# The order in which the tiles of an edge table are taken: falling width, or narrow ones among wide ones

## The chip, the cores and the metric

The kernel runs on one core of one Trainium2 chip. The metric is the device time of one execution in microseconds. Engines are called as the profile calls them: PE (TensorE, matmul), DVE (VectorE), ACT (ScalarE), POOL (GpSimd) and SP (SyncE). Each engine works through its own queue in the order in which the program was written; an instruction that waits holds everything behind it on that engine.

## What is computed

Two layers of a graph network run on `x` of 16 batches, 1024 nodes and 256 features, with one adjacency matrix `adj` of 1024 x 1024 for all batches. At most one entry in 60 of `adj` is not zero (the table below has room for 17,280 of 1,048,576).

```python
# layer 0: attention over all nodes
feats = x @ W1.T                                   # 16 x 1024 x 256
f1 = feats @ W2 + b2
coefs = softmax(leaky_relu(f1[:, :, None] + f1[:, None, :]) + adj)
h = coefs @ feats + bias2 + x
# layer 1: a score for each pair (u, v), weighted by adj
pre_u, pre_v = h @ W1[:256], h @ W1[256:]
S = sigmoid(relu(pre_u[:, :, None] + pre_v[:, None, :] + b1) @ W2 + b2)
a = einsum('buv,bud->bvd', S * adj, h)
m = einsum('uv,bud->bvd', adj, h) * h
z = beta1 * h + beta2 * (a @ Wa + ba) + beta3 * (m @ Wm + bm)
```

A score `S[u, v]` is multiplied by `adj[u, v]`, so it is needed only where `adj` is not zero. The kernel computes scores for these edges alone.

## The kernel before

Everything runs in `edge_layers`. PE does the dense work from end to end: features, attention and messages for batch after batch, and at the end the sum over `u` weighted by the scores. The scores are made beside it, by POOL, DVE and ACT, in three groups of batches (`GROUPS`: 5, 5 and 6 batches). They lie back in DRAM between the two: scores are scattered into `sa_d`, a dense 1024 x 1024 table for each group that was cleared before, and read from there as `sat` for the last matmuls.

**The table of edges.** In the first 340 us the kernel sorts the edges into pieces: up to eight edges of one row `u`, one piece to a partition, 128 pieces to a tile. There are 21 tiles. Tile `t` has `WIDTHS[t]` columns: thirteen tiles of width 8, then 7, 6, 5, 4, 3, 3, 2, 1. A column of a tile is a slot: 128 edges, one on each partition. `SLOTS` lists all 135 slots as pairs (tile, column), and this list sets the order in which every group works.

**One slot** (number `k` of a group) goes through these steps:

- `fetch` (lines 1215 to 1232): at a tile's first column, POOL issues an indirect gather of `gu`, the 128 rows `u` of `pu_d` (L1219), which then serve all columns of the tile; for every slot it issues a gather of `gv`, the rows `v` of `pw_d` (L1226). A row has 272 numbers of four bytes for each batch of the group, 5440 bytes with five batches.
- `compare` (L1255): DVE takes the maximum, and for a second half the minimum, of `gv` and `gu`; two instructions to a slot.
- `sums` (L1269): ACT adds up each batch's 272 numbers, one instruction to a batch. In the last group, every eighth slot is summed by DVE instead (L1266).
- `gates` (L1277, ACT) and L1296 (DVE) finish the scores of some 16 slots at a time.
- `scatter` (L1235): POOL scatters the 128 finished scores of a slot. Scatters wait in a list, `late`, and one or two follow each fetch.

**The rings.** `gv` has five buffers in the first two groups and six in the last, and `gu` has two in every group. The first two groups share one pool, so their rings go on across the border; the last group has a pool of its own. A new `gu` may be gathered only when L1255 has finished the last slot of the tile that held its buffer before. `AHEAD` is three slots in the first two groups and four in the last: the fetch of slot `k + AHEAD` is issued with slot `k`.

**The order.** A small timetable (`Timetable`) sets each instruction's place in its engine's queue. It gives PE's work model times, and all other work is placed relative to these. `scores` spreads a group's 135 slots evenly between two such times. The fetches with which a group begins are placed 15 us before its first slot, that is before the last fetch of the group before it:

```python
for k in range(len(SLOTS)):
    time = start + k * (end - start) / len(SLOTS)

    def first(k=k):
        for n in range(AHEAD[g]) if k == 0 else ():
            fetch(g, n)
        if k + AHEAD[g] < len(SLOTS):
            fetch(g, k + AHEAD[g])
        ...
    times.at(time - (15.0 if k == 0 else 0.0), first)
```

On DVE and ACT the instructions of the scores stand between those on which PE depends: L1054 (weights of the attention), L1081 (rows `h`), L1176 and L1195 (messages), L1357 (scores times `adj`), all on DVE, and L969, L1098, L1119 on ACT.

Of the kernel before, what the change touches and what calls it, by code (L numbers as in the profile page):

```python
# [26 lines left out]
W = 8  # L27
WIDTHS = (8,) * 13 + (7, 6, 5, 4, 3, 3, 2, 1)
TILES = len(WIDTHS)
SLOTS = [(t, s) for t, width in enumerate(WIDTHS) for s in range(width)]  # L30
HUB = 32
SEGS = P // HUB
ROUNDS = (11, 10, 6, 5, 4, 4, 4, 4, 4)
# [338 lines left out]
def edge_layers(  # L372
# [835 lines left out]

    PARTS = [16, 32, 48, 64, 80, 96, 112, 124, 131, len(SLOTS)]
    AHEAD = [n - 2 for n in GV]  # L1210
# [4 lines left out]
    def fetch(g, k):  # L1215
        t, s = SLOTS[k]
        if s == 0:
            gu = st["gu", t] = pools["gath", g].tile([P, SIZE[g] * R], F32, name="gu", bufs=2)
            nc.gpsimd.indirect_dma_start(  # L1219
                out=gu,  # L1220
                out_offset=None,
                in_=pu_d[g],
                in_offset=bass.IndirectOffsetOnAxis(ap=key_u[:, t : t + 1], axis=0),
            )
        gv = st["gv", k] = pools["gath", g].tile([P, SIZE[g] * R], F32, name="gv", bufs=GV[g])
        nc.gpsimd.indirect_dma_start(  # L1226
            out=gv,
            out_offset=None,
            in_=pw_d[g],
            in_offset=bass.IndirectOffsetOnAxis(ap=idx_v[:, t, s : s + 1], axis=0),  # L1230
        )

    def scatter(g, lg, i, k):
        t, s = SLOTS[k]
        dma = nc.gpsimd.indirect_dma_start(  # L1235
            out=sa_d[g],
            out_offset=bass.IndirectOffsetOnAxis(ap=idx_s[:, t, s : s + 1], axis=0),
            in_=lg[:, i, : SIZE[g]],
            in_offset=None,
            bounds_check=N * N - 1,  # L1240
            oob_is_err=False,
        )
        tc.declare_no_dep(dma.ins, group=f"sa{g}", reason="edges of their own")
        tc.add_to_no_dep_group(f"sa{g}", dma.ins)

    def by_batch(tile):
        return tile.rearrange("p (g r) -> p g r", r=R)

    def compare(k, half):
# [3 lines left out]
        mv = by_batch(st["gv", k])[:, :, cols]  # L1253
        mu = by_batch(st["gu", SLOTS[k][0]])[:, :, cols]
        nc.vector.tensor_tensor(mv, mv, mu, op)  # L1255
# [23 lines left out]
    def scores(g, start, end, on_vector):  # L1279

        for k in range(len(SLOTS)):
            time = start + k * (end - start) / len(SLOTS)

# [516 lines left out]
```

## Time and profile before

| what | us |
|---|---|
| median of three runs | 2098.32 |
| the three runs | 2111.71, 2086.22, 2098.32 |
| the profiled execution, its own time | 2079.83 |
| its span in the profile | 2078.1 |

From the trace: the first score (L1255) of group 0 begins at 373 us, that of group 1 at 865 us, that of group 2 at 1336 us, and the last score begins at 1875 us. A slot takes some 3.6, 3.5 and 4.0 us in the three groups.

| per core, whole span | count | busy us | mean ns |
|---|---|---|---|
| POOL L1226, gather of gv | 405 | 497.1 | 1227 |
| POOL L1235, scatter of scores | 405 | 504.1 | 1245 |
| POOL L1219, gather of gu | 63 | | 1025 (median) |
| DVE L1255, compare | 810 | 705.8 | 909 |
| ACT L1269, sums | 2058 | 856.3 | 420 |

How to read it: a row of the page has the busy time of an engine and its share of the span. In the 40 slices, each digit is the busy share of one fortieth of the span, in tenths. In the windows view, the columns behind a stretch are its length and then, for PE, PE's weight loads, DVE, ACT and POOL, the busy time with the number of instructions; behind these the granted clock, the share of the DMA engines and GB/s. In the timeline a row has the start, the time taken, the engine, the line, the operation, out<-in, shapes and count, and in brackets how long the engine was idle before it and what ended that.

The profile's times of POOL are those of making a gather's descriptors; the transfer follows. From issue to landing a gather of gv took 7.7 us in the median (4.8 to 15.0), one of gu 6.5 us (4.6 to 10.7).

### The profile page before, as it was taken

The numbers are of one execution on the slowest core, as the hardware profiler recorded it, in microseconds if no ns is written. First come the engines' busy times: TensorE is split into PE (matmuls) and PEld (weight loads), VectorE is DVE, ScalarE is ACT, GpSimd is POOL, SyncE is SP. The second block draws the span as 40 slices with busy tenths as digits, with TensorE's granted clock in tenths as the row PEclk, the third lists the DMA queues.
The fourth block names the chain that finished last, engine by engine and source line by source line (L and its number), as shares of the span: only waits on it lengthen the run. The fifth ranks groups of instructions, "written<-read, shape, count | busy, mean of one in ns | idle before, by whom it ended". The sixth has DMA issues, their size and how long they took to land.

```text
span 2078.1 us, 28958 instructions
## 1 busy us (share of the span) xinstructions
PE 2020.4 (97%) x8577; PEld 1554.9 (75%) x8577; DVE 1566.8 (75%) x2348; ACT 1371.5 (66%) x4842; POOL 1142.4 (55%) x974
## 2 busy tenths in 40 slices
PE   8999999999999999999999999899999999999998
PEld 6888887777786868677888886457677667767887
DVE  7798883677777777677878886578888888884554
ACT  4212222577777868587888777577888888885654
POOL 1121221267676777677777777666777677683000
PEclk9999999999999999999999999999999999999999
DMA  6689886788888889789999999999999999996873
GB/s 220 240 311 343 306 323 235 247 268 288 285 273 270 275 288 297 254 299 308 315 297 318 327 308 310 326 401 399 399 400 370 415 414 405 400 383 254 281 230 123
DMA packets 250007, 644.37 MB, mean 310 GB/s; under 512 B 38642, under 2 KB 139762, under 8 KB 247794
## 3 DMA queue, kind: packets, MB, share of 16 engines
q0 software_dynamic: 82016, 348.87, 47.9%
q1 hardware_dynamic: 132002, 259.36, 34.2%
q10 hardware_dynamic: 35824, 34.22, 4.7%
q8 instruction: 69, 1.13, 0.2%
q14 instruction: 96, 0.79, 0.1%
HBM read 479.56 MB, written 162.92 MB: 309 GB/s over the span
## 4 chain that ended last, share of the span: by engine, by line
PE 61%; DVE 11%; DMA 9%; ACT 8%; issue 7%; POOL 3%; ACTq 0%; POOLq 0%; DVEq 0%
PE pv L1067 18%; PE pp L1105 10%; PE pm L1165 10%; PE pzg L1370 6%; DMA gv<-pw_d,idx_v 5%; ACT gv L1269 5%; PE pf L1013 5%; DVE gv L1255 4%; PE pea L1133 4%; PE pzh L1370 3%; PE pz L1185 2%; ACT apart L1352 2%; POOL sa_d L1235 2%; DMA xh<-in_x_dram 1%; POOL gv L1226 1%
## 5 line engine op out<-in xcount | busy, mean ns | idle before, releaser
L1269 ACT ACTIVATE gv<-gv 128x272 f32<-128x272 f32 x2058 | 856.3, 420 | 313.0 <-DVE gv L1255 204.7
L1255 DVE TENSOR_TENSOR gv<-gv,gu 128x680 f32<-128x680 f32 (+1 forms) x810 | 705.8, 909 | 97.5 <-DMA gv<-pw_d,idx_v 95.5
L1226 POOL DMA_INDIRECT gv<-pw_d,idx_v x405 | 497.1, 1227 | 297.9 <-ACT gv L1269 181.5
L1235 POOL DMA_INDIRECT sa_d<-lg,idx_s x405 | 504.1, 1245 | 135.2 <-issue 108.2
L1067 PE MATMUL pv<-feats,eT 128*128 128x257 f32 x2048 | 465.5, 380 | 2.7 <-DVE eT L1054 2.0
L1165 PE MATMUL pm<-adj_sb,xh 128*128 128x512 f32 x1024 | 452.8, 595 | 2.6 <-DVE xh L1081 2.6
L1067 PEld LDWEIGHTS pv<-feats,eT 128*128 128x128 f32 x2048 | 382.9, 190 | 61.8 <-DVE eT L1054 4.2
L1269 ACT ACTIVATION_READ_ACCUMULATOR gv<-gv 128x1 f32 x2058 | 389.7, 189 | 0.0
L1370 PE MATMUL pzg<-ha_g,apart 128*128 128x256 f32 x1536 | 367.5, 382 | 19.0 <-DVE apart L1357 18.5
L1165 PEld LDWEIGHTS pm<-adj_sb,xh 128*128 128x128 f32 x1024 | 194.3, 191 | 222.4 <-issue 219.8
L1370 PEld LDWEIGHTS pzg<-ha_g,apart 128*128 128x128 f32 x1536 | 290.2, 191 | 77.2 <-DVE apart L1357 29.5
L1352 ACT COPY apart<-sat 128x640 f32<-128x640 f32 (+1 forms) x192 | 264.2, 1394 | 78.0 <-PE pzh L1370 35.5
L1357 DVE TENSOR_TENSOR apart<-apart,adj_sb 128x640 f32<-128x640 f32 (+1 forms) x192 | 165.9, 867 | 123.3 <-ACT apart L1352 123.0
L1105 PE MATMUL pp<-wuv,hT 128*128 128x272 f32 x1024 | 250.5, 395 | 6.7 <-ACT end L1119 3.8
L1105 PEld LDWEIGHTS pp<-wuv,hT 128*128 128x128 f32 x1024 | 194.7, 191 | 53.7 <-issue 6.5
L1054 DVE SCALAR_TENSOR_TENSOR eT<-row,col,grown 128x512 f32<-128x512 f32 x256 | 182.8, 745 | 27.5 <-ACT col L1000 26.8
L852 POOL DMA_INDIRECT table_d<-rec,at x52 | 57.4, 1105 | 248.4 <-DVE rec L845 151.8
L1098 ACT COPY hT<-ph 128x512 f32<-128x512 f32 x96 | 55.1, 575 | 101.0 <-PE ph L1087 100.7
L1133 PE MATMUL pea<-wa,hT 128*128 128x256 f32 x512 | 121.0, 379 | 0.0
L1185 PE MATMUL pz<-wm,mT 128*128 128x256 f32 x512 | 115.7, 379 | 0.0
L1013 PE MATMUL pf<-w1T,xT 128*128 128x257 f32 x512 | 114.1, 380 | 0.9 <-DVE xT L971 0.9
L1370 PE MATMUL pzh<-ha_g,apart 128*128 128x256 f32 x384 | 114.2, 379 | 0.0
(179 smaller groups left out, 1589.0 us busy)
## 6 DMA issues: line engine op xcount, KB each, us to landing
sa_d<-zero SPq DMA_DIRECT2D x128, 512.0 KB, 5.6
sat<-sa_d SPq DMA_DIRECT2D x128, 320.0 KB, 9.5
sat<-sa_d SPq DMA_DIRECT2D x64, 384.0 KB, 4.2
pu_d<-end SPq DMA_DIRECT2D x64, 272.0 KB, 4.3
pw_d<-end SPq DMA_DIRECT2D x64, 272.0 KB, 5.8
ha_d<-ea SPq DMA_DIRECT2D x64, 256.0 KB, 4.9
zb_d<-zb ACTq DMA_DIRECT2D x64, 256.0 KB, 7.8
xh<-in_x_dram SPq DMA_DIRECT2D x15, 1024.0 KB, 13.6
```

Of the source, the lines that this page charges most:

```text
L1013: nc.tensor.matmul(pfs[i], lhsT=st["xT"][:, h, c * P : (c + 1) * P], rhs=w1T[:, h, :], start=(h == 0), stop=(h == H - 1),)
L1054: nc.vector.scalar_tensor_tensor(st["eT", b, k, n][:, i, :], st["row"][:, cols], st["col"][:, j : j + 1], grown[:, j, cols], ALU.max, ALU. ...
L1067: nc.tensor.matmul(pv[:, : D + 1], lhsT=st["eT", b, k, j // 4][:, j % 4, i * P : (i + 1) * P], rhs=st["feats", b][:, j, :], start=(j == 0) ...
L1105: nc.tensor.matmul(pp[:, k, :R], lhsT=st["hTi", b, i][:, h, k * P : (k + 1) * P], rhs=wuv[:, side, h, :], start=(h == 0), stop=(h == H - 1),)
L1133: nc.tensor.matmul(pp[:, k, :], lhsT=st["hTi", b, i][:, h, k * P : (k + 1) * P], rhs=wa[:, h, :], start=(h == 0), stop=(h == H - 1),)
L1165: nc.tensor.matmul(pm, lhsT=held[b][:, c, h * P : (h + 1) * P], rhs=adj_sb[:, c, span], start=(c == 0), stop=(c == C - 1),)
L1226: nc.gpsimd.indirect_dma_start(out=gv, out_offset=None, in_=pw_d[g], in_offset=bass.IndirectOffsetOnAxis(ap=idx_v[:, t, s : s + 1], axis=0),)
L1235: dma = nc.gpsimd.indirect_dma_start(out=sa_d[g], out_offset=bass.IndirectOffsetOnAxis(ap=idx_s[:, t, s : s + 1], axis=0), in_=lg[:, i, : ...
L1255: nc.vector.tensor_tensor(mv, mv, mu, op)
L1269: nc.scalar.activation(one[:, j, :], one[:, j, :], AF.Copy, accum_out=lg[:, i, j : j + 1])
L1352: nc.scalar.copy(apart.rearrange("p g v -> p v g"), sat)
L1370: nc.tensor.matmul(st["pzg", g, vc][j // 4][:, j % 4, :], lhsT=apart[:, j, :], rhs=ha, start=(c == 0 and j % 2 == 0), stop=(c == C - 1 and ...
```

## The change

The order of the tiles in `SLOTS` is written out. In place of falling width, tiles of width 3, 2, 3, 4, 5, 6 and 7 stand between tiles of width 8; tile 20, of width 1, stays last.

```diff
 WIDTHS = (8,) * 13 + (7, 6, 5, 4, 3, 3, 2, 1)
 TILES = len(WIDTHS)
-SLOTS = [(t, s) for t, width in enumerate(WIDTHS) for s in range(width)]
+ORDER = (0, 1, 18, 2, 3, 19, 4, 5, 17, 6, 7, 16, 8, 15, 9, 14, 10, 13, 11, 12, 20)
+SLOTS = [(t, s) for t in ORDER for s in range(WIDTHS[t])]
```

The slots at which a tile begins:

| order | first slots of the tiles |
|---|---|
| before | 0, 8, 16, ... 96 (tiles 0 to 12), 104, 111, 117, 122, 126, 129, 132, 134 (tiles 13 to 20) |
| after | 0, 8, 16, 19, 27, 35, 37, 45, 53, 56, 64, 72, 76, 84, 89, 97, 103, 111, 118, 126, 134 |

The table, the number of slots, gathers and scatters, and the places of all other instructions in the timetable are the same.

## The prediction

> **What bounds the kernel now.** I start with the page: the engine rows, then the slices.
>
> ```profile
> PE 2020.4 (97%) x8577; PEld 1554.9 (75%) x8577; DVE 1566.8 (75%) x2348; ACT 1371.5 (66%) x4842; POOL 1142.4 (55%) x974
> ...
> PE   8999999999999999999999999899999999999998
> ...
> POOL 1121221267676777677777777666777677683000
> ```
>
> TensorE (PE) is busy for 2020.4 of 2078.1 us, so 57.7 us are all that any rearrangement could return. Whatever moves between the other engines counts only as far as it opens or closes a hole in PE. Next, therefore, the windows view, cut where the groups of scores begin, and where slot 104 of 135 comes in each group:
>
> ```profile
> 0.00:373.00 373.00, 361.89 (x1745) 305.62 (x1746) 294.15 (x565) 95.22 (x180) 70.95 (x107) 1.00 0.77 284
> 373.00:740.00 367.00, 367.00 (x1521) 274.42 (x1520) 276.63 (x442) 273.02 (x1144) 239.76 (x202) 1.00 0.84 270
> 740.00:865.00 125.00, 122.37 (x491) 88.97 (x490) 85.62 (x137) 82.12 (x352) 88.72 (x76) 1.00 0.87 294
> 865.00:1216.00 351.00, 342.37 (x1553) 278.37 (x1554) 286.20 (x472) 286.92 (x1186) 259.91 (x219) 0.99 0.90 302
> 1216.00:1336.00 120.00, 116.64 (x424) 76.68 (x424) 70.08 (x112) 74.94 (x328) 90.01 (x76) 1.00 0.94 330
> 1336.00:1751.00 415.00, 398.01 (x1500) 276.38 (x1501) 345.74 (x398) 343.24 (x1214) 286.02 (x217) 0.99 1.01 395
> 1751.00:1876.00 125.00, 117.70 (x471) 86.80 (x471) 109.17 (x125) 108.71 (x362) 94.56 (x67) 1.00 0.99 383
> ```
>
> Length less PE's busy time gives PE's holes: 11.1 us at the start, 0 and 2.6 in group 0, 8.6 and 3.4 in group 1, 17.0 and 7.3 in group 2; 7.6 remain behind 1876, mostly the last stores. The timeline of PE shows the three largest holes in the scores, and all stand at the last slot of a group:
>
> ```profile
> 864.81 3.53 PE L1165 MATMUL pm<-adj_sb,xh 128*128 128x512 f32 x4 [2.63 <-DVE xh L1081]
> ...
> 1339.92 1.12 PE L1087 MATMUL ph<-ident,xh 128*128 128x128 f32 x4 [7.28 <-DVE zb L1195]
> 1342.41 1.12 PE L1087 MATMUL ph<-ident,xh 128*128 128x128 f32 x4 [1.38 <-DVE zb L1195]
> ...
> 1875.36 3.44 PE L1370 MATMUL pzg<-ha_g,apart 128*128 128x256 f32 x8 [2.90 <-DVE apart L1357]
> ```
>
> DVE releases all of them, so DVE's timeline just before is read next. It stood at L1255, waiting for a gather, with PE's operand queued behind:
>
> ```profile
> 862.43 1.64 DVE L1255 TENSOR_TENSOR gv<-gv,gu 128x680 f32<-128x680 f32 x2 [8.37 <-DMA gv<-pw_d,idx_v]
> ...
> 1334.71 3.48 DVE L1255 TENSOR_TENSOR gv<-gv,gu 128x680 f32<-128x680 f32 x4 [14.05 <-DMA gv<-pw_d,idx_v]
> ...
> 1873.57 1.01 DVE L1255 TENSOR_TENSOR gv<-gv,gu 128x816 f32<-128x816 f32 x1 [2.87 <-DMA gv<-pw_d,idx_v]
> ```
>
> Over the whole trace DVE waits 95.5 us in 41 places for gathers. By slot (the n-th pair of L1255), the last nine slots hold 16.0 us of it in group 0, 25.1 in group 1 and 5.0 in group 2. So the narrow end does hurt; but the largest waits are at slot 134, whose tile comes last in both orders.
>
> **The change part by part.** Arithmetic, slots, scatters, bytes and the 63 gathers of gu all stay; only the places of gu's gathers move, and what their ring of two buffers waits for.
>
> *Removed from the end of each group.* From slot 104 on, before begins eight tiles (104, 111, 117, 122, 126, 129, 132, 134); after begins four (111, 118, 126, 134). A gu costs GpSimd 1.03 us plus 0.30 between instructions, and brings 128 rows of 5440 bytes, 0.70 MB (0.84 in group 2). GpSimd is the tight engine there: in 1216 to 1336 it has 90.0 us and 76 gaps of 0.3, 113 of 120 us.
>
> *Group 1 to 2, the largest term.* The timeline of GpSimd:
>
> ```profile
> 1312.48 0.96 POOL L1219 DMA_INDIRECT gu<-pu_d,key_u  x1 [0.30 <-issue]
> ...
> 1322.31 0.96 POOL L1219 DMA_INDIRECT gu<-pu_d,key_u  x1 [0.30 <-issue]
> 1323.58 0.94 POOL L1226 DMA_INDIRECT gv<-pw_d,idx_v  x1 [0.30 <-issue]
> ```
>
> The first is group 2's first gu: its look-ahead (one gu, five gv, written 15 us ahead) is queued before the last fetch of group 1. The second and third are slot 134's own. Its gv lands 11.0 us after its issue, behind 5.0 MB of look-ahead. GpSimd has run without a longer gap since 1282, when DVE held it. Of the gu issued between then and 1323.6, two (tiles 18 and 19; tile 12's takes the place of 17's) disappear: 2 x 1.33 = 2.7 us of issue, or 1.4 MB; the DMA view of 1296 to 1340 shows some 420 GB/s around 1320, so 3.3 us of transfer. The two overlap. I take 3.5 us earlier for slot 134, and about 0.5 us off the second hole: -4. Bounds: -8.7 if both holes go, 0 if the look-ahead alone sets the landing.
>
> *Group 0 to 1.* Here slot 134's gu waits for L1255 of slot 133 in either order (ring of two, with the next group's first gu in between). From the end of slot 133 at 852.7 to the landing at 862.4 are 9.7 us that stay. What goes are the waits before, 4.4 and 3.2 us at slots 131 and 132, which made DVE late. DVE is idle for a quarter of the time anyway and takes back part; of the 2.6 us hole I take 2: -2 (0 to -2.6).
>
> *End of group 2.* Three gu wait there in before (one took 2.66 us of idle and 3.80 of issue at 1836.87); after has two gu, neither held. I take 2 of the 2.9 us hole: -2 (0 to -4.4, with the two holes of 0.6 and 0.7 before it).
>
> *Added among the wide tiles.* A tile behind a narrow one takes the buffer of the tile before the narrow one. Behind width 2 (tile 4, slot 37) its gu waits for slot 34. Groups 0 and 1 issue it three slots ahead, so DVE reaches slot 37 three slots of 3.6 us later, less 1.7 of its own work: 9.1 us. Needed are 1.3 us for gu, 1.0 for the issue of gv, and gv's landing (median 7.7 from issue): about 9.0 to 10. So DVE waits 0 to 2 us. Group 2 asks four slots ahead, and there widths 2 and 3 (slots 37, 19, 56) wait on the slot directly. Nearest rows for what a wait costs PE: 5.44 us of DVE wait at 461.44 opened no hole at all, 4.26 at 1683.41 opened 1.15. I take 0 in groups 0 and 1 (the dense rows are the nearest) and 1 + 0.5 + 0.5 = +2 in group 2; bounds 0 and +9 (2.9, the price at 1875.36, at three places). Group 1's first part gets four more gu, 5.3 us on a GpSimd filled for 260 + 67 of 351 us; I take +1 (-2 to +3). Queued behind a held gu are its gv, the next gv, and scatters nobody waits for until the group ends.
>
> *A rule against it.* The trace has gv landing 7.7 us after issue. The Trainium skill, "DMA: Bandwidth & Descriptors", section "Anatomy of one DMA — SWDGE (gpsimd) path", fits 2.0 us plus bytes over 436e3 per us: an estimate of 3.6 us for 0.70 MB. By that, three slots of look-ahead would cover everything in either order and the sum would be 0. The row shows twice that under load, and 95.5 us of waits.
>
> Sum: -4 - 2 - 2 + 2 + 1 = **-5 us**. The profiled execution took 2079.8 us (span 2078.1 and 1.7 around it), so 2075 by its own measure. That run lies 18 us under the median of the three shown, 2098.3, and 6 under their lowest. On the median: **2093**. The three spread over 25 us, so within 1% (21 us) counts as no change here.
>
> **Rivals.**
> *The handover, not the narrow tiles, makes the holes.* For: slot 134 keeps its place, its look-ahead and its 9.7 us chain. Against: GpSimd shows only 0.3 us gaps before 1312. Then the ends give 0, the inside +0: 2098.
> *Slower: the ring of gu holds GpSimd inside the groups.* Place: slot 37 of each group, 19 and 56 of group 2. Price: 2.9 us of PE each, as at 1875.36, 14.5; less half of the gains, 4: +10, 2108. It decides if the gv behind the held gu lands over about 10 us after the slot it waited for; group 2's landings of 11 us (1862.90 to 1873.57) speak for it, the holeless 461.44 against. To reach 1% each place would have to cost some 5 us.
> *The whole end was a lag of GpSimd.* Then all holes behind slot 120 go: 2.6 + 8.7 + 4.4, and 1.3 at 893, which a late DVE starts: -17, 2081. Against: half the tile starts remain, and DMA runs at 0.99 there.
>
> **How the numbers follow.** Forecast 0.50, handover 0.19, slower 0.20, whole lag 0.11. Range: the terms' bounds give -18 to +16 about 2098, and a median of three whose runs spread over 25 us may itself move by some 10; both ends seldom meet, so 2070 to 2115. Faster by over 1% needs the whole lag and some holes more: 0.08. Slower by over 1% is the outer part of the slower case: 0.11. Within: 0.81.
>
> **What would show it.** Right: the hole at the end of group 1 falls to about 4 us; DVE's waits at slots 128 to 133 vanish; a wait of gu for L1255 appears at slot 37; the sum of DVE's waits for gathers falls from 95.5 to some 75. Wrong: PE holes over 2 us inside a group, or 14 us still at the last slot. The forecast fails most easily if group 1, whose GpSimd is full already, takes up the moved gathers worse than its end did.

## The result, and the profile after

The change makes the kernel a little slower: 2109.73 us in the median of 22 runs (2096.59 to 2115.23), against 2099.42 of 22 runs of the kernel before in the same sessions. The ratio is 1.0041 [1.0026, 1.0056], or +8.6 us [+5.5, +11.8]; the two medians themselves stand 10.3 apart. The forecast was -5.

The two profiled executions stand 31.8 us apart (2111.66 and 2079.83), and only about a quarter of that is the change: the execution of before that was profiled lies under all of its 22 timed runs (lowest 2086.22), that of after near its median. The two traces can't be subtracted, so most readings below were repeated with pairs from one chip.

From the page of after, the engine rows and two slice rows:

```profile
PE 2034.5 (96%) x8577; PEld 1561.5 (74%) x8577; DVE 1565.9 (74%) x2348; ACT 1371.2 (65%) x4842; POOL 1141.8 (54%) x974
...
PE   8999999999999999999889999899999999999998
...
POOL 1122221366677667667667776666677676683000
```

DVE, ACT and POOL work as long as they did, to 1 us. New are two slices with an 8 in PE's row, just behind 1000 us, in group 1. The windows view of after, with the cuts that the prediction used:

```profile
865.00:1216.00 351.00, 325.79 (x1444) 261.23 (x1443) 264.94 (x434) 264.50 (x1100) 248.12 (x205) 0.97 0.86 285
1216.00:1336.00 120.00, 114.79 (x447) 82.67 (x446) 80.88 (x134) 86.98 (x369) 85.31 (x72) 0.97 0.85 293
1336.00:1751.00 415.00, 395.81 (x1457) 268.40 (x1456) 325.85 (x377) 324.06 (x1161) 283.71 (x220) 0.99 1.00 391
1751.00:1876.00 125.00, 119.03 (x477) 88.27 (x476) 111.21 (x128) 111.18 (x367) 90.55 (x68) 1.00 1.02 398
```

Length less PE's busy time gives 25.2 us of holes in 865 to 1216, where before had 8.6. The other rows have 5.2, 19.2 and 6.0, near before's 3.4, 17.0 and 7.3. So the loss arises in the middle of group 1. (After runs some 30 us late by the end, so its own slots are used from here on: slots 35 to 104 of group 1 lie at 979 to 1247 and hold 26.7 us; in before, at 975 to 1216, 7.3.)

At the ends of the groups the change did what it was expected to do. The timeline of PE in after, and of DVE just before, at the end of group 1:

```profile
1368.49 0.81 PE L1088 MATMUL ph<-ident,xh 128*128 128x128 f32 x4 [4.29 <-DVE zb L1196]
1370.98 1.12 PE L1088 MATMUL ph<-ident,xh 128*128 128x128 f32 x4 [1.69 <-DVE zb L1196]
```

```profile
1363.28 3.48 DVE L1256 TENSOR_TENSOR gv<-gv,gu 128x680 f32<-128x680 f32 x4 [14.86 <-DMA gv<-pw_d,idx_v]
```

The hole fell from 7.28 to 4.29 us, though DVE's wait for slot 134 stayed at 14.86 (14.05 in before). At the last slot of group 0 the hole went from 2.63 to 0.6, and at that of group 2 from 2.90 to none.

### The profile page after: what moved, and what is told of

It reads as the page before. It is cut to its first block, busy times and chain, and to the rows that moved or that the text cites. A ratio compares the mean times of both kernels' runs of the same rounds, so it can differ in the third digit from the quotient of the medians.

```text
span 2109.9 us, 28964 instructions
## 1 busy us (share of the span) xinstructions
PE 2034.5 (96%) x8577; PEld 1561.5 (74%) x8577; DVE 1565.9 (74%) x2348; ACT 1371.2 (65%) x4842; POOL 1141.8 (54%) x974
## 4 chain that ended last, share of the span: by engine, by line
PE 53%; DVE 15%; ACT 11%; issue 9%; DMA 8%; POOL 3%; another core or an unknown queue 1%; ACTq 0%; POOLq 0%; DVEq 0%; SPq 0%
PE pv L1068 15%; PE pm L1166 8%; PE pp L1106 7%; PE pzg L1371 7%; ACT gv L1270 7%; DVE gv L1256 7%; DMA gv<-pw_d,idx_v 6%; PE pea L1134 4%; PE pf L1014 3%; PE pzh L1371 3%; ACT apart L1353 2%; PE pz L1186 2%; DVE apart L1358 2%; DVE eT L1055 1%; POOL gv L1227 1%
## 5 line engine op out<-in xcount | busy, mean ns | idle before, releaser
L1256 DVE TENSOR_TENSOR gv<-gv,gu 128x680 f32<-128x680 f32 (+1 forms) x810 | 705.3, 907 | 97.9 <-DMA gv<-pw_d,idx_v 91.4
L1227 POOL DMA_INDIRECT gv<-pw_d,idx_v x405 | 479.0, 1183 | 321.1 <-ACT gv L1270 203.6
L1236 POOL DMA_INDIRECT sa_d<-lg,idx_s x405 | 521.6, 1288 | 129.5 <-issue 106.4
L1371 PE MATMUL pzg<-ha_g,apart 128*128 128x256 f32 x1536 | 367.4, 382 | 20.8 <-DVE apart L1358 12.3
L1106 PE MATMUL pp<-wuv,hT 128*128 128x272 f32 x1024 | 254.7, 399 | 14.5 <-ACT end L1120 5.0
L1055 DVE SCALAR_TENSOR_TENSOR eT<-row,col,grown 128x512 f32<-128x512 f32 x256 | 182.7, 745 | 36.8 <-ACT col L1001 25.5
L1220 POOL DMA_INDIRECT gu<-pu_d,key_u x63 | 75.7, 1202 | 79.5 <-PE pv L1068 41.0
```

The source lines that it names most:

```text
L1055: nc.vector.scalar_tensor_tensor(st["eT", b, k, n][:, i, :], st["row"][:, cols], st["col"][:, j : j + 1], grown[:, j, cols], ALU.max, ALU. ...
L1106: nc.tensor.matmul(pp[:, k, :R], lhsT=st["hTi", b, i][:, h, k * P : (k + 1) * P], rhs=wuv[:, side, h, :], start=(h == 0), stop=(h == H - 1),)
L1227: nc.gpsimd.indirect_dma_start(out=gv, out_offset=None, in_=pw_d[g], in_offset=bass.IndirectOffsetOnAxis(ap=idx_v[:, t, s : s + 1], axis=0),)
L1236: dma = nc.gpsimd.indirect_dma_start(out=sa_d[g], out_offset=bass.IndirectOffsetOnAxis(ap=idx_s[:, t, s : s + 1], axis=0), in_=lg[:, i, : ...
L1371: nc.tensor.matmul(st["pzg", g, vc][j // 4][:, j % 4, :], lhsT=apart[:, j, :], rhs=ha, start=(c == 0 and j % 2 == 0), stop=(c == C - 1 and ...
```

## The experiments

In the tables, "holes" is window length less PE's busy time, cut at the kernel's own slots; "gather waits" are DVE's waits at the compare (L1255, or the same line where an edit has moved it, as L1256) for a gather of gv. A view names what ended a wait by the semaphore records in the trace, and only five traces have these whole: before's first profile and the four from chip 1 hold 30,700 such records each, all others 21,300 to 22,800. There a wait for a gather can stand under "issue" or another name. So "all idle" is given beside it: DVE's whole idle time just before the compare. In the five whole traces the two differ by at most 2 us over slots 35 to 104 of group 1. Every ratio is against the kernel before on the same chip. Five chips were met, and before takes a different time on each: 2080.4 us on chip 1, 2099.6 on chip 0, 2102.1 on chip 4, 2116.0 on chip 10, 2118.8 on chip 7.

The theory that came out of the first comparison: POOL has no spare time in group 1, so tiles that begin two or three slots apart make it late there, and DVE waits. Its rivals: the loss is of another group; it comes from the wide tiles that were moved too; it is the ring of gu that holds POOL; or it isn't of the change at all, and before's profile was a lucky one. Some expectations below speak of more holes than the tables (some 40 us for after, where its windows give 26.7); the tables go by the windows.

**Which group.** The lists of slots are made per group.

```diff
-SLOTS = [(t, s) for t in ORDER for s in range(WIDTHS[t])]
+FALLING = tuple(range(len(WIDTHS)))
+ORDERS = (FALLING, ORDER, FALLING)        # only_g1
+ORDERS = (ORDER, FALLING, ORDER)          # only_g02
+LISTS = [[(t, s) for t in order for s in range(WIDTHS[t])] for order in ORDERS]
```

> The mixed order of the tiles in group 1 alone; groups 0 and 2 take falling width. Theory A (group 1, where GpSimd is full, is the place of the loss: in the trace of the changed kernel PE loses 25 us there at 865 to 1216, against 9 before): as slow as the whole change or slower, +6 to +12 us. Theory B (the loss is the ring of gu holding GpSimd, which shows in group 2, where gu waited 9.8 us at slot 37): +-3 us. Theory C (no place: the two profiles differ mostly by chance between executions): +-3 us here, and +-3 us in the other kernel.

> The mixed order in groups 0 and 2, falling width in group 1. Theory A: no slower than before, 0 to -5 us, since the ends of groups 0 and 2 lose their holes. Theory B: +4 to +10 us, with holes in PE around slots 37 and 56 of group 2. Theory C: +-3 us.

| chip 10 | ratio | group 1, slots 35 to 104: holes, gather waits, all idle | group 2, slots 35 to 60: holes | end of group 2: holes |
|---|---|---|---|---|
| only_g1 | 1.002 [0.9993, 1.0046] | 27.7, 20.3, 25.5 | 1.1 | 6.8 |
| only_g02 | 0.9999 [0.9971, 1.0027] | 24.2, 5.9, 12.2 | 4.8 | 4.4 |

Neither total can be told from no change, so the times don't say which group it is; the stages say more. DVE's idle time before the compare is double where group 1 has the mixed order (25.5 against 12.2); the holes differ by 3.5. Group 2 gains 2.4 us at its end and pays 3.7 at slots 35 to 60, so it gains nothing.

**The handover.** The falling order, with the look-ahead of the next group placed 13 us ahead, so that POOL issues it behind the last fetch of the group before it.

```diff
-            times.at(time - (15.0 if k == 0 else 0.0), first)
+            times.at(time - (13.0 if k == 0 else 0.0), first)
```

> Falling width as before; a group's look-ahead is placed 13 us before its first slot and not 15, so that on GpSimd the last fetch of the group before stands ahead of it (two neighbours change places at each of the two borders, nothing else). If the handover makes the holes of 2.6 us and 7.3 + 1.4 us at the last slots: -5 to -10 us. If a late GpSimd makes them: 0 to -2 us. If the next group's first slots then come late: +2 to +5 us.

0.9998 [0.9974, 1.0022]: no gain. Against before_look (below, the same chip) the holes from slot 104 of group 1 to slot 35 of group 2 shrink from 11.3 to 6.9 us, but those from group 0 to 1 grow from 10.1 to 15.5: the late fetches are now those of the group that begins.

**The same kernels again.** Before and after, unchanged, profiled on other chips.

> The kernel before, once more, for a second profile. Its first profile was of an execution of 2079.8 us, 20 us under its median. If the changed kernel's holes in group 1 are its own, this profile shows 8 to 14 us of holes in group 1 up to slot 104; if they come and go with the execution, it shows some 20.

> The changed kernel once more, on the same chip as the kernels beside it and with a second profile. If its loss is its own and not of one execution: +6 to +12 us against the kernel before; PE holes in group 1 of 20 us or more at slots 35 to 60 and 18 or more at 60 to 104 (the three profiles of falling width in that group have 1.7, 13.9 and 16.7, and 9.6, 14.3 and 16.1).

before_look took 1.0007 [0.9978, 1.0035] of before, and after_look 1.0033 [1.0005, 1.006]. In group 1, slots 35 to 104, before now had 23.4 us of holes, not 7.3. So most of the 19 us that the first comparison showed there was no property of the order. Gather waits in that stretch were 11.1 (8.7 in the first profile), and 16.5 in after_look (22.0); all idle was 18.1 (8.7), and 19.9 in after_look (22.2). So between these two, which are of different chips, neither number keeps the orders apart. One place does: at slot 37 of group 1, where tile 4 begins two slots behind tile 19, DVE waits 3.8 to 5.1 us in all four traces with the mixed order there and all scatters (after, after_look, after_third, only_g1), and 0 to 1.8 us in the five with falling width (before, before_look, before_third, last_first_13, only_g02).

**Which tiles.** Only the three narrow tiles moved in, or only the four wider ones.

```diff
 # narrow3: tiles 18, 19, 17 (3, 2, 3 columns) among the wide ones, the rest falling
+ORDER = (0, 1, 18, 2, 3, 19, 4, 5, 17, 6, 7, 8, 9, 10, 11, 12, 13, 14, 15, 16, 20)
 # wide4: tiles 16, 15, 14, 13 (4 to 7 columns) among the wide ones, the narrow ones last
+ORDER = (0, 1, 2, 3, 4, 5, 6, 7, 16, 8, 15, 9, 14, 10, 13, 11, 12, 17, 18, 19, 20)
```

> Of the change only the tiles of width 3, 2 and 3 go among the wide ones, to the places they have there (slots 16, 35 and 53); widths 7, 6, 5 and 4 stay at the end in falling order, then tile 20. If these three tiles make the loss by their extra starts close together: as slow as the whole change, +6 to +12 us. If the loss is the sum of all starts moved into the full part of group 1: half of it, +2 to +5 us.

> Of the change only the tiles of width 7, 6, 5 and 4 go among the wide ones (from slot 64 on); widths 3, 3, 2 and 1 stay last. Starts in slots 35 to 60 are those of falling width (three), where the change has five. If the narrow tiles with their starts two or three slots apart make the loss: within 3 us of before, with holes at slots 35 to 60 of group 1 as in falling width (1.7 to 17) . If every start moved out of the end costs the same: +3 to +6 us.

narrow3 1.0033 [1.0012, 1.0054], as after_look on the same chip; wide4 1.0006 [0.9983, 1.0029]. Gather waits in slots 35 to 104 of group 1 are 14.5 and 7.9, but all idle is 20.9 and 19.2, so the profiles don't tell the two apart. The times point to the three narrow tiles. They don't settle it: wide4 was timed on chip 7, where the whole change was not, and its interval reaches to +6 us.

**POOL's load.** In group 1 every second scatter is left out, so those scores stay zero in the output. The same edit in both orders.

```diff
-                late.extend(lambda i=i: scatter(g, lg, i, k0 + i) for i in range(k1 - k0))
+                late.extend(
+                    lambda i=i: scatter(g, lg, i, k0 + i)
+                    for i in range(k1 - k0)
+                    if g != 1 or (k0 + i) % 2 == 0
+                )
```

> The mixed order, but in group 1 every second slot's scores are not scattered: 67 of 135 scatters, with them about 1.5 us of GpSimd for every second slot, are left out, and those scores stay zero. Theory A (GpSimd is full in group 1 and the moved gathers of gu come on top): the holes of PE at slots 35 to 104 of group 1 fall from some 40 us to under 15, and the difference to the falling order with the same scatters left out is within 3 us. Theory B (a buffer of gu held by the tile before): the holes stay above 30 and the difference stays at +6 to +12 us.

> Falling width, with the same scatters of group 1 left out. Theory A: faster than before by 10 us or more, since PE's holes in group 1 are GpSimd's there too. Theory B: -3 to 0 us.

half_mixed took 2083.30 us and half_falling 2083.06, against 2099.58 of before: 16 us less in both, and 0.2 us between the orders. The ratios are 0.9913 [0.9887, 0.9940] and 0.9932 [0.9910, 0.9954]: no difference shows between the orders, and a loss of the change's size would. The windows of slots 35 to 104 of group 1, first half_mixed, then half_falling:

```profile
985.00:1228.00 243.00, 234.02 (x1130) 199.27 (x1128) 198.00 (x333) 199.69 (x814) 143.09 (x121) 1.00 0.91 313
```

```profile
984.00:1226.00 242.00, 233.34 (x1128) 199.05 (x1127) 197.49 (x332) 200.05 (x813) 143.29 (x117) 1.00 0.90 308
```

Holes of 9.0 and 8.7 us. The same stretch with all scatters, from a pair on chip 4, first before_third (falling), then after_third (mixed):

> Falling width on the same chip: no difference to itself; the profile gives the holes to compare with.

> The changed kernel beside before_third and skip_third on one chip, for a profile of each under the same conditions. +5 to +10 us; more holes at slots 35 to 104 of group 1 than before_third by 5 to 15 us; 4 more at slots 35 to 60 of group 2 and 3 fewer at its last slots.

```profile
990.00:1241.00 251.00, 237.05 (x1125) 200.80 (x1123) 197.01 (x332) 199.79 (x810) 179.68 (x152) 0.99 0.89 298
```

```profile
983.00:1246.00 263.00, 235.72 (x1109) 196.70 (x1108) 197.16 (x332) 198.70 (x807) 184.23 (x155) 0.99 0.87 292
```

Holes of 14.0 and 27.3 us; the stretch is 12 us longer. POOL's busy time and 0.30 us for each instruction fill 225 of 251 us in before_third and 179 of 243 in half_mixed. With that slack no cost of the order is left. The edit takes away the scatters' transfers too; that POOL's time is what counts, and not these, is argued: the DMA engines' share is no lower without them (0.91 and 0.90, against 0.89 and 0.87). (The pair's totals: 1.0017 [0.9997, 1.0037] and 1.0028 [1.0011, 1.0045].)

The ring of gu does hold POOL in half_mixed, at slot 37 of group 1:

```profile
985.68 1.34 POOL L1220 DMA_INDIRECT gu<-pu_d,key_u  x1 [4.31 <-DVE gv L1256]
```

This is the wait that the prediction looked for, and there it opens no loss: holes are 2.1 us at slots 35 to 60, against 1.6 in half_falling.

What DVE waits for there, from the view of waits of before_third and then of after_third (columns: total us, times, longest):

```profile
DVE gv L1255 <- DMA gv<-pw_d,idx_v: 6.9, 8, 1.6
DVE eT L1054 <- ACT col L1000: 6.9, 3, 3.2
```

```profile
DVE gv L1256 <- DMA gv<-pw_d,idx_v: 18.9, 11, 5.1
DVE eT L1055 <- ACT col L1001: 7.2, 3, 3.2
```

All idle is 11.7 us in before_third and 27.6 in after_third. One such place can be followed. The timeline of POOL in after_third, where tile 19 (slot 35) and, two slots later, tile 4 (slot 37) begin:

```profile
969.65 1.24 POOL L1227 DMA_INDIRECT gv<-pw_d,idx_v  x1 [4.85 <-ACT gv L1270]
...
973.96 1.16 POOL L1220 DMA_INDIRECT gu<-pu_d,key_u  x1 [0.30 <-issue]
975.42 2.69 POOL L1227 DMA_INDIRECT gv<-pw_d,idx_v  x1 [0.30 <-issue]
978.41 1.84 POOL L1227 DMA_INDIRECT gv<-pw_d,idx_v  x1 [0.30 <-issue]
980.56 1.96 POOL L1236 DMA_INDIRECT sa_d<-lg,idx_s  x1 [0.30 <-issue]
982.83 1.00 POOL L1236 DMA_INDIRECT sa_d<-lg,idx_s  x1 [0.31 <-issue]
984.13 1.62 POOL L1220 DMA_INDIRECT gu<-pu_d,key_u  x1 [0.30 <-issue]
986.07 1.25 POOL L1227 DMA_INDIRECT gv<-pw_d,idx_v  x1 [0.30 <-issue]
```

From 969.65 on every gap is the 0.30 us that follows any instruction: no gu waits for the ring of gu. But POOL isn't only full. Just before, it stood for 4.85 us until ACT gave back a buffer of gv, so it could not work ahead, and three of the rows take 2.69, 1.84 and 1.96 us where the means are 1.23 and 1.25. Then DVE and PE:

```profile
993.65 1.64 DVE L1256 TENSOR_TENSOR gv<-gv,gu 128x680 f32<-128x680 f32 x2 [5.08 <-DMA gv<-pw_d,idx_v]
997.05 1.64 DVE L1256 TENSOR_TENSOR gv<-gv,gu 128x680 f32<-128x680 f32 x2 [1.75 <-DMA gv<-pw_d,idx_v]
...
999.21 0.71 DVE L1118 TENSOR_TENSOR end<-pp,bu 128x544 f32<-128x544 f32 x1
```

```profile
999.98 1.97 PE L963 MATMUL pt<-ident,xh 128*128 128x128 f32 x8 [3.04 <-DVE end L1118]
```

DVE waits 5.08 and 1.75 us, its `end` comes late, and PE has a hole of 3.04. Of after_third's holes over 0.3 us in that stretch, 8.0 us in all end within 10 us after a wait of over 1 us at the compare; in before_third none do (on chip 10 it is 10.4 us in only_g1 and 4.9 in before_look). For the other 5 of the 13 us the traces show no such link. By the means of before's table, three slots with two gu ask POOL for 3 x (1.23 + 1.25 + 0.60) + 2 x 1.33 = 11.9 us, and get 3 x 3.5 = 10.5. Every start makes POOL late, but between starts eight slots apart it catches up 0.4 us a slot; between starts two apart it can't. A rival to this is the ring of gv: over slots 35 to 104 of group 1 POOL waits 12.3 us for ACT at L1226 in before_third and 23.1 us at L1227 in after_third. A longer look-ahead or more buffers of gv would have tested it; neither was tried.

**Moving scatters away from the starts.** If the crowding at a start is all, POOL need only leave out the scatter there and catch up later. Three ways, each in both orders:

```diff
+                opens = k + AHEAD[g] < len(SLOTS) and SLOTS[k + AHEAD[g]][1] == 0
 # calm: up to 28 scatters may wait in group 1, 12 elsewhere
+                pops = 0 if opens else 2 if len(late) > (2 if g == 1 else 1) * PARTS[0] - 4 else 1
 # skip: two at a time as soon as 13 wait
+                pops = 0 if opens else 2 if len(late) > PARTS[0] - 4 else 1
 # even: as calm, but two at most in every third slot (every second in group 2)
+                waiting = (12, 28, 12)[g]
+                pops = 0 if opens else 2 if len(late) > waiting and k % (2 if g == 2 else 3) == 1 else 1
-                for _ in range(min(len(late), 2 if len(late) > PARTS[0] - 4 else 1)):
+                for _ in range(min(len(late), pops)):
```

In these kernels some scatters of group 1 stand behind the first reads of its table, and the scores that they bring are missing from those reads.

> Falling width. A slot whose fetch opens a tile lets no scatter out, and in group 1 two go out at a time only from 29 waiting on, not from 13: GpSimd has no scatter behind a gu, and 14 scatters of group 1 slip into group 2, where it has room. Theory A (GpSimd is full in group 1, and the gathers behind a tile's first column come late): -5 to -12 us. If GpSimd's time is not the cause: 0 to +3 us.

> The same rule for scatters on the mixed order. Theory A: what the change lost in group 1 comes back, -4 to -12 us against before, and the holes of PE at slots 35 to 104 of group 1 fall from 31 to 41 us to under 20. If the loss is the ring of gu: +4 to +10 us as without the rule.

> The mixed order; a slot whose fetch opens a tile lets no scatter out, and the next ones make up for it (two at a time from 13 waiting, as before), so that each group keeps its number of scatters. If the crowding at a tile's start is the cause (a scatter behind each gu and gv while DVE already waits): 0 to +3 us against before and holes at slots 35 to 60 of group 1 under 12 us. If the sum of GpSimd's work in group 1 is the cause, wherever it stands: +6 to +10 us as without the rule.

> Falling width with the same rule. If the crowding at a tile's start is the cause: -3 to -8 us, since before has it too at 21 starts a group. If only the sum of GpSimd's work counts: 0 to -2 us.

> The mixed order; no scatter with a gu, group 1 lets up to 28 wait (12 in the others), and what waits too long goes out as a second scatter in every third slot (every second in group 2) and not in every slot: some 20 scatters of group 1 go to group 2 without a burst there. If GpSimd's work in group 1 is the cause and the burst of the earlier rule was its fault: -2 to -8 us against before, holes at slots 35 to 60 of group 1 under 8 us and at the start of group 2 as in before (9 to 15 us).

> The same rule on falling width: -6 to -12 us if it works as in the mixed order; it may beat both kernels.

> The mixed order with no scatter in a slot that opens a tile, on the same chip. If crowding at the starts is the cause: holes at slots 35 to 104 of group 1 within 5 us of before_third; if the sum of GpSimd's work is: as many as after_third. In either case some us more at the start of group 2, where the last scatters of group 1 now stand behind reads of the same table and wait for them (15 us in skip_mixed).

| kernel, chip | ratio | holes, group 1, slots 35 to 60 | slots 60 to 104 | group 1, slot 104, to group 2, slot 35 |
|---|---|---|---|---|
| before_third, 4 | 1.0017 [0.9997, 1.0037] | 4.8 | 9.2 | 12.2 |
| after_third, 4 | 1.0028 [1.0011, 1.0045] | 11.2 | 16.0 | 7.8 |
| skip_third (mixed), 4 | 1.0011 [0.9990, 1.0031] | 6.0 | 17.9 | 14.7 |
| skip_falling, 1 | 1.0062 [1.0050, 1.0074] | 1.2 | 8.1 | 14.4 |
| skip_mixed, 1 | 1.0033 [1.0020, 1.0046] | 2.1 | 6.8 | 12.7 |
| calm_falling, 7 | 1.0149 [1.0117, 1.0182] | 3.4 | 11.5 | 38.8 |
| calm_mixed, 7 | 1.0115 [1.0092, 1.0138] | 3.2 | 12.0 | 35.2 |
| even_falling, 1 | 1.0293 [1.0277, 1.0309] | 1.0 | 7.2 | 55.8 |
| even_mixed, 1 | 1.0243 [1.0228, 1.0259] | 5.0 | 6.6 | 45.4 |

The crowded stretch, slots 35 to 60, does become calm. But the scatters that were put off are paid for at the end of the group, where they wait for the table's readers. From the view of POOL's waits, calm_falling:

```profile
POOL sa_d L1235 <- DMA sat<-sa_d: 32.9, 6, 6.4
```

and even_falling:

```profile
POOL sa_d L1235 <- DMA sat<-sa_d: 68.6, 11, 8.5
```

So a scatter on POOL is not free to wait, as the prediction had it ("scatters nobody waits for until the group ends"): the end of the group comes soon, and everything POOL put off is there at once. How much of the loss is crowding at the starts and how much POOL's sheer load is not settled: in skip_third slots 35 to 60 fall from 11.2 to 6.0 us, but slots 60 to 104 stay at 17.9, and its total of 23.9 lies nearer to after_third's 27.2 than to before_third's 14.0. No kernel of the study is faster than before, apart from the two that leave out scatters.

A third buffer for gu, which would have taken its ring away by itself, wasn't tried.

## Why the prediction was wrong

It put the time at 2093 us and the change at -5, by five terms. Same-chip pairs give them sizes; single profiles do not.

- **End of group 2, -2: right.** 7.3 to 7.9 us of holes from slot 104 in the falling order (before, before_look, before_third), 4.4 in every mixed one: -3.
- **Group 0 to 1, -2: right in sign.** 8.0 to 3.9 us on chip 4: -4, beyond the bound of -2.6, which counted the one hole of before's first profile.
- **Group 1 to 2, -4: right.** 12.2 to 7.8 us on chip 4: -4.4, and the hole at slot 134 fell to "about 4 us" as said in after (4.29) and after_third (4.66), though in after_look it is 6.81. The handover rival was half right: DVE's wait of 14 to 15 us for slot 134 didn't move.
- **Inside group 2, +2: right.** +2.2 us on chip 4 and +3.7 on chip 10 at slots 35 to 60, and some +1.5 at slots 60 to 104. Here the ring of gu does hold POOL, as foreseen: the gu of slot 56 waits 3.44 us, and that of slot 37, in the timeline of POOL in after:

```profile
1496.52 3.78 POOL L1220 DMA_INDIRECT gu<-pu_d,key_u  x1 [9.78 <-DVE gv L1256]
```

- **Inside group 1, 0 for slot 37 and +1 for four more gu: the step that failed.** In holes it is +13 us on chip 4 (14.0 to 27.2) and +4 on chip 10 (23.4 to 27.7), beyond the stated bound of +3. By the stretch's own length, which also holds what PE loses at a halved clock, it is +12 us on chip 4 (251 to 263) and +6 to +11 on chip 10 (268 in only_g1; 257, 261 and 262 in before_look, only_g02 and last_first_13). The working looked for a wait of the ring of gu at slot 37, had DVE wait 0 to 2 us for it, priced that by "5.44 us of DVE wait at 461.44 opened no hole", and took 0. DVE waits 3.8 to 5.1 us there, and in none of the four traces does that gu wait for its ring. What the traces show in its place is a POOL with little time left that comes late, and the working had that number too (260 + 67 of 351 us), but asked it for four gu on average, and not for two of them within three slots. In group 0 the ring does hold POOL at slot 37 (1.65 to 3.20 us) and PE's timeline shows no hole in the 15 us behind it (after, after_look, after_third), so the 0 was right there. The row at 461.44 is of group 0, where POOL has 240 of 367 us: near in kind, far in load. The last sentence of the prediction, that group 1 might take up the moved gathers "worse than its end did", is what happened.

With chip 4's sizes the sum is -3 - 4 - 4 + 3 + 13 = +5, against +5.9 [+2.3, +9.5] measured there. That the two agree is partly luck: the two executions whose holes were counted stand only 2.7 us apart (2109.51 and 2106.81), and the pair's medians 1.7. Nor is it a full account: in the same pair the holes of slots 0 to 104 of group 0, for which there is no term, fell from 5.3 to 1.1 us. With chip 10's size of the last term it would be -4, and there after itself was not timed (the ratios of only_g1 and only_g02 add up to +0.2%, some +4 us). The size of the failed term is known only as +4 to +13, and that POOL's lateness makes all of it is not shown. The slower rival had the time (2108) but for the greater part not the mechanism: at its places the ring costs PE something in group 2 alone.

Of the signs that were to show it right, the hole at the end of group 1 fell to 4.29. DVE's waits at slots 128 to 133 of group 1 fell from 11.0 to 3.4 us, but did not vanish. A wait of gu at slot 37 appeared in groups 0 and 2, and not in group 1. The sum of DVE's gather waits was to fall from 95.5 to about 75: it was 91.4 in after, yet 97.2 in before_third and 77.6 in after_third, the very fall that was forecast, while PE lost. The sum counts waits at the narrow end, most of which cost PE little, like those in full stretches, some of which it pays for. Both signs of being wrong came: DVE still waited 14.86 us at the last slot, and PE has holes over 2 us inside the groups. The second says little, since before_look and before_third have such holes too (3.22 at 1087, 3.50 at 1028).

The range (2070 to 2115) held the time, since it left room for a median that differs from the one shown. (The terms' bounds add up to -18 and +12, not to the +16 given with it.)

## What the runs showed that was not expected

**Waits without a name.** In the views of waits, some rows name no releaser: "issue" or "remote". Added up over the whole trace, DVE has 0 us of these in before's first profile, and 0 to 0.5 in the four kernels profiled on chip 1, the fast one. In all other traces it has 31 to 115 us in 26 to 55 places, whatever the order. These are the traces in which semaphore records are missing, so many such rows are waits whose end was not recorded. One of them, from the timeline of DVE in after, and what PE makes of it:

```profile
1073.57 0.17 DVE L1079 RECIPROCAL inv<-pv 128x1 f32<-128x1 f32 x1 [6.56 <-remote]
```

```profile
1075.72 1.97 PE L963 MATMUL pt<-ident,xh 128*128 128x128 f32 x8 [7.24 <-DVE end L1118]
```

Here something else is seen too. The semaphore that ends this wait is PE's own: the trace has its update at 1073.54, 5 us after the end of PE's last matmul (1068.48), and three more updates in the 0.3 us behind it. In before's first profile every such update follows a matmul's end within 0.05 us, but for two at the very end of the run. So after's largest hole in group 1 is not of POOL. Why the updates come late the traces don't say. The whole traces are those of the fast executions (2079.83 us, and chip 1, where before takes 2080), and in the falling order, all scatters issued, the holes of slots 35 to 104 in group 1 are 7.3 us in before's first profile and 14.0 to 24.2 in the others. Whether one makes the other was not tested. On chip 1 a late POOL may cost less: there skip_mixed had 14.0 us of gather waits in slots 35 to 104 against 8.1 of skip_falling, with the same holes (8.9 and 9.3), and was 8 us faster in total. The change itself, with its scatters as they are, was never run on that chip; that it loses there too is open.

**A short hole can halve the clock.** The windows of before around the hole of 2.63 us at the end of group 0; the third column from the right is the granted clock:

```profile
858.00:862.00 4.00, 4.00 (x21) 3.28 (x19) 0.00 (x0) 0.00 (x0) 2.81 (x3) 1.00 0.76 296
862.00:865.00 3.00, 0.37 (x2) 0.22 (x2) 2.54 (x5) 0.85 (x5) 0.00 (x0) 0.93 0.01 1
...
865.00:869.00 4.00, 4.00 (x6) 1.67 (x7) 3.52 (x7) 3.97 (x20) 2.10 (x2) 0.63 0.19 27
```

Behind the hole PE gets 0.63 of its clock over four microseconds (0.50 in each of 865 to 866 and 866 to 867), so the hole costs, by estimate, another 0.37 x 4 = 1.5 us, as busy time. Not every such hole does it: after_third's of 2.41 us at 1102 is followed by no such stretch. The Trainium skill, "TensorE: Matmul & The Clock Gate", "Part 1: The HAM clock gate (the "warmup" mystery)", tells of a half clock after an idle window of some 3.4 us; here less was enough. Before's first profile has four such stretches within the scores, after's has eight. This is part of why PE's busy time differs between the two pages (2020.4 and 2034.5), and a count of holes alone misses it.

## What to carry to other kernels

Where an engine is nearly full, price an added instruction by what it asks for within the look-ahead's few slots as well as by the average of the stage; and take the row that prices a wait from a stage with the same load. Spreading short pieces of work evenly did not help where the engine that starts them had little slack: here the full stretch was in the middle, and the narrow tiles were moved into it from an end that was no worse. Profile the kernel before a second time, on another chip, before a trace that is faster than the median is taken for its behaviour. Where a trace names no end for many waits, compare whole idle times and not the named ones.
